# A graph layer's node phase: when turn, product and rows of a group are made, and when gathered rows are stored

## The chip, the cores and the metric

The kernel runs on one core of one Trainium2 chip. The metric is the device time of one execution in microseconds (us). Three runs of the kernel before took 4763.48, 4764.75 and 4766.40 us; the median, 4764.75 us, is its time here.

A core has five engines with queues of their own: PE (matrix products and transposes, with PEld for its weight loads), DVE (vector work), ACT (scalar functions), POOL (here: it issues the gathers) and SP (it issues most other DMAs). An engine takes its instructions in the order of its queue. What orders the engines against each other are semaphores.

## The reference, cut to what matters

There are 12500 nodes with 128 features and 400000 edges, sorted by destination. One graph attention layer (GATv2, 8 heads) and a feed-forward block follow a normalised input:

```python
h = jnp.maximum(_layernorm(x, axis=-1), 0.0)
# inside the layer, with n1 = layernorm(h) * ln1_g + ln1_b
x_l = (n1 @ W_l).reshape(n, H, C)
x_r = (n1 @ W_r).reshape(n, H, C)
m = leaky_relu(x_l[src] + x_r[dst] + e, 0.2)        # e from the edge attributes
alpha = einsum('ehc,hc->eh', m, att)                 # softmax over the edges of a destination
out = segment_sum(x_l[src] * a[:, :, None], dst)     # then bias, residual, feed-forward
```

The change concerns the first part of the work alone: from `x` to `h`, and from `h` to the table of rows `x_l`, which the edges gather by `src`.

## The kernel before, in words

The nodes are padded to 98 tiles of 128. The program has a **node phase**, in which `h` and `x_l` are made for all nodes, and an **edge phase**, which takes the edges 512 at a time: POOL gathers rows of `x_l` from memory (L938), PE, ACT and DVE work out scores and sums. The edge phase needs `x_l` of all nodes in memory, since any edge may point to any node.

In the node phase a *group* is four tiles (25 groups, the last of two tiles; `qs`). A group goes through small steps. The statistics: `x_stats` (DVE, L500: two instructions a tile), `x_mean` (DVE), a square root on ACT (L778) and a reciprocal on DVE (L776) for all groups of a round together, `relu` (ACT, L513: it makes `h` and sums it up), `h_mean` (DVE), `h_square` (ACT, L536), `h_var` (DVE). The product: `h_turn` (PE, L523: four transposes into a PSUM tile `tp`), `h_turned` (L528: the copy to SBUF, on DVE for odd groups, on ACT for even ones), `product` (PE, L549, into a PSUM tile `lr`), `x_l` (DVE, L556: one instruction a tile, and the group's store by SP, L568). For the first group six more steps make its `x_r` (`xr_steps`, L570); `x_r` of the other groups is made in the edge phase.

Beside the groups the phase **gathers raw rows**: for 28 places of the edge list, whose edges are needed in the edge phase, four gathers each (112 in all) bring rows of the input `x` into an SBUF buffer `raw` (`raw_gather`, POOL, L293), and SP stores the buffer in memory (`raw_store`, L305). There are 12 such buffers, so the gathers of place k + 12 wait until the store of place k has landed.

The order is written out by hand. The program is a loop of **rounds** r (L753). In a round come first the raw gathers and stores that are due, then constants (round 3 weights; rounds 9 to 11 and on: differences of destinations, on ACT in rounds 11 to 17, stored by SP in round 18; round 13 constants of the edge phase, DVE; round 15 `fits`, a check on DVE with a small product on PE), then the reciprocals and roots, then the statistics (`sums`, L715: group r - late at step `late`), then the products (`products`, L723), then the first group's `x_r`. Each engine's queue holds its instructions in this order.

Before the change the statistics of group g start in round g, and its turn comes in round `turn_at[g]`, which is 13 + 2g // 3 or, if that is later, g + 5: three groups in two rounds, from 13 on to 29. Copy, product and `x_l` follow one, two and three rounds behind the turn. The stores of places 0 to 4 come three rounds behind their gathers (rounds 3, 4, 5, 6 and 8); place 5 is stored in round 17, and from there one place a round, the last eight of all in the last round, 33 (L749 to L751).

Of the kernel before, what the change touches and what calls it, by code (L numbers as in the profile page):

```python
# [13 lines left out]
F32 = mybir.dt.float32  # L14
# [6 lines left out]
PSUM = bass.MemoryType.PSUM  # L21

P = 128
# [11 lines left out]
KU = 2  # L35
U = KU * P
UP = 2
QP = 4
RU = 14
# [9 lines left out]
XW = P + H  # L49
CX = XW // H  # L50
GN = 4
# [5 lines left out]
RAW_MORE = 6  # L57
RAW_SHIFT = 8
RAW_STEPS = 12
TURN_AT = 13  # L60
BUSY = 5
RAW_BUFS = 12
FREE = 5
BIG = 2.0**126
CAP = 2.0**120

# [66 lines left out]
def raw_pairs(nt, n_edges):  # L133

    n_pr = -(-n_edges // (UP * U))
    at = [xr_round(t, nt, n_edges) + XR_STEPS + 1 for t in range(GN, nt, GN)]
    at = at[:-1] + [r + RAW_SHIFT for r in at[:RAW_MORE]]
    return [(r + RAW_STEPS + AHEAD + 1, r) for r in at if r + RAW_STEPS + AHEAD + 2 < n_pr]
# [11 lines left out]
def tile_gnn(  # L150
# [23 lines left out]
    nc = tc.nc  # L174
# [23 lines left out]
    raw = [{"c": c, "i": i, "round": r, "n": UP * KU} for i, (c, r) in enumerate(raw_pairs(NT, n_edges))]  # L198
# [33 lines left out]
    pre = ExitStack()  # L232
    build = pre.enter_context(tc.tile_pool(name="build", bufs=1))
    rng = pre.enter_context(tc.tile_pool(name="rng", bufs=1))
    node = pre.enter_context(tc.tile_pool(name="node", bufs=3))
    once_ps = pre.enter_context(tc.tile_pool(name="once_ps", bufs=1, space=PSUM))
    tp_ps = pre.enter_context(tc.tile_pool(name="tp_ps", bufs=3, space=PSUM))
    lr_ps = pre.enter_context(tc.tile_pool(name="lr_ps", bufs=3, space=PSUM))


# [9 lines left out]
    def load_weights():  # L250
        nc.scalar.dma_start(wl_sb, w_l)
        nc.scalar.dma_start(wr_sb, w_r)
        nc.scalar.dma_start(g1_c, column(ln1_g))
        nc.scalar.dma_start(b1n_c, column(ln1_b))
# [19 lines left out]
    def load_first():  # L274
        nc.scalar.dma_start(
            src_first,
            bass.AP(tensor=src.tensor, offset=src.offset + raw[0]["c"] * UP * KU, ap=[[NCH * K, P], [1, UP * KU]]),
        )
# [12 lines left out]
            )  # L291

    def raw_gather(d):  # L293
        d["x"] = node.tile([P, UP * KU, P], F32, name="raw", bufs=RAW_BUFS)
        for j in range(d["n"]):
            nc.gpsimd.indirect_dma_start(  # L296
                out=d["x"][:, j, :],
                out_offset=None,
                in_=x,
                in_offset=bass.IndirectOffsetOnAxis(  # L300
                    ap=src_raw[:, d["i"], j : j + 1] if d["i"] > 0 else src_first[:, j : j + 1], axis=0
                ),
            )

    def raw_store(d):  # L305
        nc.sync.dma_start(raw_dram[d["i"], :, 0 : d["n"], :], d["x"][:, 0 : d["n"]])

    def load_x(t0, n):
        if n > 0:
            nc.sync.dma_start(h_sb[:, t0 : t0 + n, :], x_t[:, t0 : t0 + n, :])  # L310
# [104 lines left out]
    def from_first():  # L415
        nc.vector.tensor_copy(df, dc)
        nc.vector.tensor_scalar(nf, df[:, 0:EP:U], -1.0, None, op0=OP.mult)
        nc.vector.memset(dlr[:, :, :, OW:OS], 0.0)
# [15 lines left out]
    def fits():  # L434
# [44 lines left out]
    qs = [  # L479
        {"t0": t, "n": n, "ts": slice(t, t + n), "h": h_sb[:, t : t + n, :], "mean": mean_sb[:, t : t + n]}  # L480
        for t, n in quads
    ]
# [45 lines left out]
    def h_turned(by, odd):  # L528
        def turned(d, r):
            if d["t0"] // GN % 2 == odd:  # L530
                d["hT"] = node.tile([P, GN, P], F32, name="hT", bufs=4)
                by(d["hT"][:, 0 : d["n"]], d["tp"][:, 0 : d["n"]])

        return turned
# [9 lines left out]
    def h_var(d, r):  # L544
        nc.vector.tensor_scalar(root_of(d, r, 1), d["ssq"], 1.0 / P, EPS, op0=OP.mult, op1=OP.add)

    xls = [build.tile([P, GN, XW], F32, name=f"xl{i}") for i in range(4)]

    def product(d, r):  # L549
        d["lr"] = lr_ps.tile([P, GN, P], F32, name="lr")  # L550
# [19 lines left out]
    def xr_steps(pool, bank):  # L570


        def tile_of(d, name, i):
            d[name] = pool.tile([P, GN, P], F32, name=f"xr_{i}")
            return d[name][:, 0 : d["n"]]

        def norm(d):
            off = pool.tile([P, GN], F32, name="xr_off")[:, 0 : d["n"]]
            nc.vector.tensor_mul(off, d["mean"], d["r1"])
            hn = tile_of(d, "hn", 0)  # L580
            for t in range(d["n"]):
# [17 lines left out]

        def times(d):  # L600
            d["b"] = bank()
            for t in range(d["n"]):
                nc.tensor.matmul(
                    d["b"][:, t * P : (t + 1) * P], d["hT"][:, t, :], wr_c.rearrange("p c h -> p (c h)"),
                    start=True, stop=True,
                )

        def keep(d):
            n = d["n"]
            d["xr"] = pool.tile([P, GN, XW], F32, name="xr_rows")[:, 0:n, 0:P]  # L610
# [97 lines left out]
    def clear(g):  # L708
# [3 lines left out]
                empty.rearrange("p h f -> p (h f)")[:, None, :].to_broadcast([P, GT, SW]),  # L712
            )

    sums = (  # L715
        (2, x_mean),
        (4, h_mean),
        (6, h_var),
        (0, x_stats),
        (3, relu),  # L720
        (5, h_square),
    )
    products = (  # L723
        (1, h_turned(nc.vector.tensor_copy, 1)),
        (1, h_turned(nc.scalar.copy, 0)),
        (3, x_l),
        (2, product),
        (0, h_turn),
    )
    turn_at = [TURN_AT + 2 * g // 3 for g in range(len(qs))]  # L730
    turn_at = [max(at, g + 5) for g, at in enumerate(turn_at)]
    XL_AT = turn_at[0] + 3
    END = turn_at[-1] + 4
    first_xr = xr_steps(node, lambda: once_ps.tile([P, GN * P], F32, name="w_ps"))
    with tc.manual_schedule():
        load_first()
        make_identity(nc, ident)
        for t in xls:
            nc.vector.memset(t[:, :, P:], 1.0)
        load_weights()  # L740
        load_x(0, min(GN, NT))
        load_raw()
        load_x(GN, min(3 * GN, NT - GN))
        for t in range(4 * GN, NT, 14):
            load_x(t, min(14, NT - t))
        load_dst()
        load_consts()
        nc.vector.memset(empty, 0.0)
        nc.vector.memset(empty[:, :, C + 1 : SH], CAP)  # L749
        rows_at = [min(i * 5 // 4, END - 1) for i in range(len(raw))]  # L750
        kept_at = [at + 3 if i < FREE else min(XL_AT + 1 + i - FREE, END) for i, at in enumerate(rows_at)]  # L751
        assert all(kept_at[i - RAW_BUFS] <= rows_at[i] for i in range(RAW_BUFS, len(raw)))
        for r in range(max(END, 13 + RU // UP, 16) + 1):  # L753
            if r == 0:
                count_up()
            for d, at, kept in zip(raw, rows_at, kept_at):
                if r == at:
                    raw_gather(d)
                if r == kept:
                    raw_store(d)  # L760
            if r == 3:
                weights()
            if r == 9:
                last_of_units()
            if r == 10:
                from_first()
            if 0 <= r - 11 < RU // UP:
                differ(r - 11)
            if r == 11 + RU // UP:
                keep_differences()  # L770
            if r == 13:
                edge_constants()
            if r == 15:
                fits()
            for t in slots(r - 2):
                nc.vector.reciprocal(t, t)  # L776
            for t in slots(r - 1):
                nc.scalar.activation(t, t, AF.Sqrt)  # L778
            for late, f in sums:
                if 0 <= r - late < len(qs):  # L780
                    f(qs[r - late], r)
            for late, f in products:
                for d, at in zip(qs, turn_at):
                    if r == at + late:
                        f(d, r)
            if 0 <= r - XL_AT < len(first_xr):
                first_xr[r - XL_AT](qs[0])
        clear(0)
    pre.close()

# [1112 lines left out]
```

## Time and profile before

| what | us |
|---|---|
| median of three runs | 4764.75 |
| the profiled execution | 4750.58 |
| its span | 4748.8 |
| first raw gather on POOL starts | 3.42 |
| last raw gather starts | 215.80 |
| last `x_l` instruction of the node phase starts | 220.14 |
| first gather of the edge phase starts | 224.40 |
| first product of a full edge round on PE (L996) | 237.66 |

The profile is of one execution; times count from the start of its span, and the execution has 1.8 us around the span. In lists of instructions each line has the start and the duration in us, engine, line, operation, tiles and shapes, the count, and in brackets how long the engine was idle before it and what ended that ("issue": nothing that the profile shows; "remote": a releaser that it doesn't name). In tables of windows each engine has its busy time and, behind an x, its instructions. In groups by line, the first pair of numbers is busy us and mean ns of one, the rest idle time before them.

### The profile page before, as it was taken

How to read it: one execution, taken by the hardware profiler on the slowest of the kernel's cores; microseconds unless marked ns; L12 is line 12 of the kernel's file. 1: busy time of each engine (PE TensorE's matmuls, PEld its weight loads, DVE VectorE, ACT ScalarE, POOL GpSimd, SP SyncE). 2: the span in 40 equal slices, each digit the busy share in tenths (PEclk: the TensorE clock that was granted, in tenths of full speed). 3: DMA queues.
4: the chain of work that ended last, by engine and by line, in shares of the span. 5: the costliest groups of instructions: out<-in, count | busy, mean ns of one | idle time of the engine just before them, and what ended most of it. 6: DMA issues, size and time to landing. Idle time of an engine off the chain costs nothing.

```text
span 4748.8 us, 63213 instructions
## 1 busy us (share of the span) xinstructions
PE 3809.5 (80%) x18462; PEld 2367.6 (50%) x18463; DVE 2975.0 (63%) x6288; ACT 2166.6 (46%) x4744; POOL 2960.0 (62%) x3140
## 2 busy tenths in 40 slices
PE   0368888888888888888888888888888888888888
PEld 0335555555555555555554555555555555555555
DVE  2647677676676666666666666666666656656655
ACT  3524344344445445445444454444454454444443
POOL 5466666666666666666666666666666666666663
PEclk9779898888899989998998998999899899889898
DMA  5546666555554444444444444444444444444442
GB/s 137 174 120 153 157 160 151 139 137 134 127 116 96 92 93 89 96 84 92 94 95 92 92 101 92 85 95 84 92 99 93 91 90 88 90 89 85 96 89 54
DMA packets 625454, 502.71 MB, mean 106 GB/s; under 512 B 320318, under 2 KB 522157, under 8 KB 624861
## 3 DMA queue, kind: packets, MB, share of 16 engines
q1 hardware_dynamic: 524381, 281.11, 25.5%
q0 software_dynamic: 100000, 217.32, 21.7%
q8 instruction: 153, 2.51, 0.2%
q14 instruction: 200, 1.64, 0.1%
q10 hardware_dynamic: 720, 0.13, 0.0%
HBM read 432.28 MB, written 65.83 MB: 105 GB/s over the span
## 4 chain that ended last, share of the span: by engine, by line
PE 63%; DVE 12%; issue 10%; another core or an unknown queue 7%; ACT 2%; DMA 1%; SPq 0%; POOL 0%; DVEq 0%; ACTq 0%
PE acc L1059 16%; PE ab L1020 14%; PE z L996 13%; PE pt_ps L1045 10%; PE z L992 7%; DVE rec L1026 2%; DVE ea L979 2%; DVE m L1015 2%; DVE own L1068 2%; PE acc L1343 1%; ACT p L1037 1%; PE acc L1368 1%; DVE rec L1074 1%; DVE ne L985 0%
## 5 line engine op out<-in xcount | busy, mean ns | idle before, releaser
L938 POOL DMA_INDIRECT xs<-xl_dram,src_sb x3009 | 2847.6, 946 | 1622.2 <-issue 785.6
L1037 ACT ACTIVATE p<-ab,rec 128x256 f32<-128x256 f32 x1563 | 656.1, 471 | 1254.3 <-DVE rec L1026 781.6
L1059 PE MATMUL acc<-xs,pt 128*128 128x136 f32 x6250 | 1007.4, 307 | 162.7 <-issue 111.7
L1068 DVE TENSOR_TENSOR own<-acc,diag 128x272 f32<-128x272 f32 x782 | 341.5, 437 | 1268.5 <-remote 373.2
L1059 PEld LDWEIGHTS acc<-xs,pt 128*128 128x128 f32 x6250 | 901.5, 214 | 193.5 <-issue 136.1
L996 PE MATMUL z<-ea,zw 64*128 64x512 f32 x1564 | 934.7, 678 | 36.0 <-issue 11.2
L1020 PE MATMUL ab<-m,negrep 128*128 128x512 f32 x1564 | 895.8, 655 | 15.0 <-issue 13.7
L1050 ACT COPY pt<-pt_ps 128x512 f32<-128x512 f32 x782 | 456.3, 584 | 974.3 <-remote 346.9
L992 PEld LDWEIGHTS z<-ident,xs 128*128 128x128 f32 x3125 | 399.7, 151 | 708.1 <-issue 323.1
L992 PE MATMUL z<-ident,xs 128*128 128x128 f32 x3125 | 518.6, 291 | 288.0 <-remote 79.6
L1045 PEld LDWEIGHTS pt_ps<-ident,p 128*128 128x128 f32 x3125 | 357.6, 150 | 739.6 <-issue 668.9
L1045 PE MATMUL pt_ps<-ident,p 128*128 128x128 f32 x3125 | 563.0, 306 | 96.4 <-issue 61.6
L979 DVE TENSOR_SCALAR ea<-dl,nid 32x516 f32<-32x516 bf16 x782 | 582.0, 744 | 32.1 <-issue 6.8
L1015 DVE TENSOR_TENSOR m<-z,zs 128x512 f32<-128x512 f32 x782 | 532.5, 681 | 94.1 <-issue 45.9
L1026 DVE TENSOR_REDUCE rec<-ab 128x2 f32<-128x512 f32 x781 | 533.4, 683 | 71.3 <-remote 35.4
L1010 ACT ACTIVATE zs<-z 128x512 f32<-128x512 f32 x782 | 475.8, 608 | 45.5 <-issue 23.3
L1003 PE MATMUL ab<-ne,farw 64*128 64x512 bf16 x782 | 318.3, 407 | 106.3 <-ACT p L1037 76.4
L1074 DVE TENSOR_REDUCE rec<-own 128x34 f32<-128x272 f32 x782 | 340.8, 436 | 26.8
L996 PEld LDWEIGHTS z<-ea,zw 64*128 64x128 f32 x1564 | 245.3, 195 | 198.2 <-issue 178.2
L1020 PEld LDWEIGHTS ab<-m,negrep 128*128 128x128 f32 x1564 | 276.4, 216 | 30.4 <-issue 30.0
L296 POOL DMA_INDIRECT raw<-in_x,src_raw x112 | 105.9, 946 | 102.5 <-DMA raw_dram<-raw 67.7
L985 DVE TENSOR_SCALAR ne<-dl,nid 96x512 bf16<-96x512 bf16 x391 | 150.0, 384 | 13.4 <-DMA dl<-du_dram 1.0
(232 smaller groups left out, 2195.3 us busy)
## 6 DMA issues: line engine op xcount, KB each, us to landing
ea<-in_ea_t SPq DMA_DIRECT2D x392, 128.0 KB
ea_s<-in_ea_t SPq DMA_DIRECT2D x98, 512.0 KB
xs<-xl_dram,src_sb POOLq DMA_INDIRECT x3009
dl<-dc_dram SPq DMA_DIRECT2D x392, 66.0 KB
state<-rec SPq DMA_DIRECT2D x1563, 9.0 KB
state<-empty SPq DMA_DIRECT2D x28, 504.0 KB
f_st<-state SPq DMA_DIRECT2D x46, 288.0 KB
dl<-du_dram SPq DMA_DIRECT2D x392, 32.0 KB
```

The source lines that it names most:

```text
L938: nc.gpsimd.indirect_dma_start(out=xs[:, j, :], out_offset=None, in_=xl_dram, in_offset=bass.IndirectOffsetOnAxis(ap=src_sb[:, c * KP + j ...
L979: nc.vector.tensor_scalar(d["ea"][rs].rearrange("p (a b) -> p a b", b=OW), d["dl"][rs].rearrange("p (a b) -> p a b", b=OS)[:, :, 0:OW], ni ...
L992: nc.tensor.matmul(z[:, j * P : (j + 1) * P], d["xs"][:, j, 0:P], ident, start=(j == 0), stop=False, is_transpose=True)
L996: nc.tensor.matmul(z[:, :e], d["zw"][rs], d["ea"][rs, :e], start=False, stop=True)
L1010: nc.scalar.activation(d["zs"][:, :e], d["z"][:, :e], AF.Copy, scale=SLOPE)
L1015: nc.vector.tensor_tensor(d["m"][:, :e], d["z"][:, :e], d["zs"][:, :e], op=OP.max)
L1020: nc.tensor.matmul(d["ab"][:, :e], negrep.rearrange("p n h -> p (n h)"), d["m"][:, :e], start=False, stop=True)
L1026: nc.vector.tensor_reduce(d["rec"][:, :, CX], d["ab"].rearrange("p (u e) -> p u e", e=U), AX.X, OP.min)
L1037: nc.scalar.activation(d["p"][:, us], d["ab"][:, us], AF.Exp, bias=d["rec"][:, i, CX:SH], scale=-1.0)
L1045: nc.tensor.transpose(d["pt_ps"][:, js], d["p"][:, js], ident)
L1050: nc.scalar.copy(d["pt"][:, :e], d["pt_ps"][:, :e])
L1059: nc.tensor.matmul(d["acc"][:, i, :], d["pt"][:, j * P : (j + 1) * P], d["xs"][:, j, :], start=(j == js[0]), stop=(j == js[-1]),)
```

## The change

The products join the statistics in one list with fixed distances. The turn of group g comes in round g + 4, its copy in g + 5, its product in g + 7, its `x_l` in g + 8: one group a round, the first `x_l` in round 8 and the last in round 32. Within a round `x_l`, `product` and `h_turn` stand behind the copy of odd groups and ahead of `relu`; the copy of even groups on ACT stands last. Every place's raw rows are stored three rounds behind their gathers: places 5 to 15 in rounds 9, 10, 11, 13, 14, 15, 16, 18, 19, 20 and 21, the last four in rounds 33 to 36. The loop has 37 rounds and had 34. The steps for the first group's `x_r` start in round 8 and started in round 16. The PSUM pool of `tp` has two tiles and had three; the buffers of `x_l` are three and were four. No instruction is added or taken away, and the sizes of all are the same.

```diff
-    tp_ps = pre.enter_context(tc.tile_pool(name="tp_ps", bufs=3, space=PSUM))
+    tp_ps = pre.enter_context(tc.tile_pool(name="tp_ps", bufs=2, space=PSUM))
...
-    xls = [build.tile([P, GN, XW], F32, name=f"xl{i}") for i in range(4)]
+    xls = [build.tile([P, GN, XW], F32, name=f"xl{i}") for i in range(3)]
...
-    sums = (
+    node_stages = (
         (2, x_mean),
         (4, h_mean),
         (6, h_var),
         (0, x_stats),
+        (5, h_turned(nc.vector.tensor_copy, 1)),
+        (8, x_l),
+        (7, product),
+        (4, h_turn),
         (3, relu),
         (5, h_square),
+        (5, h_turned(nc.scalar.copy, 0)),
     )
-    products = (
-        (1, h_turned(nc.vector.tensor_copy, 1)),
-        (1, h_turned(nc.scalar.copy, 0)),
-        (3, x_l),
-        (2, product),
-        (0, h_turn),
-    )
-    turn_at = [TURN_AT + 2 * g // 3 for g in range(len(qs))]
-    turn_at = [max(at, g + 5) for g, at in enumerate(turn_at)]
-    XL_AT = turn_at[0] + 3
-    END = turn_at[-1] + 4
+    LAST = 8
...
-        rows_at = [min(i * 5 // 4, END - 1) for i in range(len(raw))]
-        kept_at = [at + 3 if i < FREE else min(XL_AT + 1 + i - FREE, END) for i, at in enumerate(rows_at)]
...
-        for r in range(max(END, 13 + RU // UP, 16) + 1):
+        rows_at = [i * 5 // 4 for i in range(len(raw))]
+        for r in range(max(max(len(qs), 9) + LAST + 1, max(12 + RU // UP, 16), rows_at[-1] + 4)):
...
-                if r == kept:
+                if r == at + 3:
                     raw_store(d)
...
-            for late, f in sums:
+            for late, f in node_stages:
                 if 0 <= r - late < len(qs):
                     f(qs[r - late], r)
-            for late, f in products:
-                for d, at in zip(qs, turn_at):
-                    if r == at + late:
-                        f(d, r)
-            if 0 <= r - XL_AT < len(first_xr):
-                first_xr[r - XL_AT](qs[0])
+            if 0 <= r - LAST < len(first_xr):
+                first_xr[r - LAST](qs[0])
```

More of the change, by code (lines that the diff above doesn't have):

```diff
@@ L59 @@
 RAW_STEPS = 12
-TURN_AT = 13
 BUSY = 5
-RAW_BUFS = 12
-FREE = 5
 BIG = 2.0**126
@@ L293, in raw_gather @@
     def raw_gather(d):
-        d["x"] = node.tile([P, UP * KU, P], F32, name="raw", bufs=RAW_BUFS)
+        d["x"] = node.tile([P, UP * KU, P], F32, name="raw", bufs=12)
         for j in range(d["n"]):
@@ L749, in tile_gnn @@
         nc.vector.memset(empty[:, :, C + 1 : SH], CAP)
-        rows_at = [min(i * 5 // 4, END - 1) for i in range(len(raw))]
-        kept_at = [at + 3 if i < FREE else min(XL_AT + 1 + i - FREE, END) for i, at in enumerate(rows_at)]
-        assert all(kept_at[i - RAW_BUFS] <= rows_at[i] for i in range(RAW_BUFS, len(raw)))
-        for r in range(max(END, 13 + RU // UP, 16) + 1):
+        rows_at = [i * 5 // 4 for i in range(len(raw))]
+        for r in range(max(max(len(qs), 9) + LAST + 1, max(12 + RU // UP, 16), rows_at[-1] + 4)):
             if r == 0:
                 count_up()
-            for d, at, kept in zip(raw, rows_at, kept_at):
+            for d, at in zip(raw, rows_at):
                 if r == at:
                     raw_gather(d)
-                if r == kept:
+                if r == at + 3:
                     raw_store(d)
```

## The prediction

> **What bounds the kernel now.** The page comes first, to see how much of the run the change can touch.
>
> ```profile
> span 4748.8 us, 63213 instructions
> ...
> PE   0368888888888888888888888888888888888888
> ...
> L296 POOL DMA_INDIRECT raw<-in_x,src_raw x112 | 105.9, 946 | 102.5 <-DMA raw_dram<-raw 67.7
> ```
>
> A slice of the PE row is 118.7 us (4748.8 / 40). PE is full from the third or fourth slice on; the change edits the node phase alone, which lies in the first two. The third line is the other user of that phase: 112 gathers of raw rows on POOL (four more have a group of their own). They cost POOL 106 us, and POOL waited 67.7 us for a buffer to be stored. So I read the phase by windows, cut where the timeline changes its pace.
>
> ```profile
> core 0: us, PE busy (x) PEld busy (x) DVE busy (x) ACT busy (x) POOL busy (x), PEclk, DMA share, GB/s
> ...
> 19.00:99.00 80.00, 3.80 (x8) 1.46 (x8) 9.80 (x62) 18.67 (x74) 52.53 (x56) 1.00 0.58 141
> 99.00:131.00 32.00, 0.00 (x0) 0.00 (x0) 26.96 (x120) 32.00 (x134) 0.00 (x0) 1.00 0.00 1
> 131.00:165.00 34.00, 23.67 (x158) 21.93 (x158) 28.86 (x147) 32.08 (x132) 13.50 (x15) 0.90 0.59 185
> 165.00:180.00 15.00, 2.50 (x12) 2.54 (x13) 4.30 (x20) 5.68 (x21) 9.22 (x10) 0.57 0.40 118
> ...
> 190.00:203.00 13.00, 1.97 (x11) 1.76 (x9) 3.23 (x13) 6.75 (x30) 9.25 (x10) 0.67 0.37 109
> ```
>
> Two paces show. From 99 to 165 ACT is busy 64 of 66 us: ACT sets the pace. From 19 to 99, 165 to 180 and 190 to 203 no engine but POOL is busy, and few instructions are issued: **slow stretches**. The timeline tells what they wait for.
>
> ```profile
> 73.76 0.18 DVE L505 BATCH_NORM_AGGREGATE n_stats<-s 128x2 f32<-128x6 f32 x1 [2.44 <-issue]
> 84.93 0.20 ACT L515 ACTIVATION_READ_ACCUMULATOR h_sb<-h_sb,n_m,roots_sb 128x1 f32 x1 [0.90 <-issue]
> 86.33 0.49 ACT L515 ACTIVATE h_sb<-h_sb,n_m,roots_sb 128x128 f32<-128x128 f32 x1 [1.20 <-issue]
> 98.96 0.40 ACT L540 ACTIVATE sq<-h_sb,mean_sb 128x128 f32<-128x128 f32 x1 [1.23 <-ACT sq L540]
> 165.10 0.18 DVE L505 BATCH_NORM_AGGREGATE n_stats<-s 128x2 f32<-128x6 f32 x1 [0.34 <-DVE s L504]
> 177.50 3.61 PE L552 MATMUL lr<-wl_c,hT 128*128 128x128 f32 x16 [12.58 <-remote]
> 218.45 0.37 ACT L532 COPY hT<-tp 128x256 f32<-128x256 f32 x1 [8.83 <-remote]
> ```
>
> Inside a stretch an instruction comes every 1.4 us (ACT at 84.93 and 86.33), with no releaser in the profile. POOL's own timeline has the other half.
>
> ```profile
> 3.42 1.10 POOL L296 DMA_INDIRECT raw<-in_x,src_first  x1 [0.22 <-DMA src_first<-in_src]
> 88.77 0.95 POOL L296 DMA_INDIRECT raw<-in_x,src_raw  x1 [0.30 <-issue]
> 142.86 0.95 POOL L296 DMA_INDIRECT raw<-in_x,src_raw  x1 [53.15 <-DMA raw_dram<-raw]
> 157.25 0.94 POOL L296 DMA_INDIRECT raw<-in_x,src_raw  x1 [4.68 <-DMA raw_dram<-raw]
> 176.02 0.95 POOL L296 DMA_INDIRECT raw<-in_x,src_raw  x1 [0.30 <-issue]
> 207.03 0.95 POOL L296 DMA_INDIRECT raw<-in_x,src_raw  x1 [3.83 <-DMA raw_dram<-raw]
> 224.40 0.95 POOL L938 DMA_INDIRECT xs<-xl_dram,src_sb  x1 [7.66 <-DMA raw_dram<-raw]
> 283.17 0.95 POOL L938 DMA_INDIRECT xs<-xl_dram,src_sb  x1 [0.30 <-issue]
> ```
>
> Gathers issue every 1.25 us (0.95 + 0.30). Suppose that something behind them needs 1.4 us for each (an estimate, fitted to these rows). A run of 68 from 3.42 would be worked off at 3.42 + 95.2 = 98.6; the last wait of ACT ends at 98.96. A run of 16 from 157.25 (to 176.02) ends at 179.7 by this; PE came back at 177.50. A run of 8 from 207.03 ends at 218.2; ACT's wait ended at 218.45. The stretch that follows 157.25 began at 165.10, 7.9 us or some seven gathers in. So my rule for this phase: **a run of n gathers without a pause makes a slow stretch from about 7.5 us after its start to 1.4 n us after it.** POOL stood still from 89.7 to 142.9 because the sixth store waits in SP's queue for round 17: that is what bought the fast window 99 to 142.
>
> **The change part by part.** What it removes, adds and moves: no arithmetic changes. Moved forward are 25 turns, copies, products and rows, the first group's x_r, 25 stores of x_l and 23 stores of raw rows. The stores are all on SP: x_l's now go one a round ahead of the loads and stores that the constants add to that queue (lu in round 9, the differences in round 18), which nothing needs before the edge phase or the check of round 15.
>
> *Rounds 0 to 8.* Stores 0 to 4 keep their rounds, so 17 groups of four gathers go out as before, POOL stops at 89.7 and the stretch ends at 99. Inside it rounds 5 to 8 now carry two copies and four row instructions more on DVE. At 1.4 us each (row 86.33) that is 8.4 us; what is left at 99 goes at the fast pace, so I take 5: round 9 starts at 102 and not at 97. Bounds: 1 us, if only busy time counts, and 8 us, if PE in the loop holds up whole rounds as it does in the edge phase's first stretch:
>
> ```profile
> 47.86 0.16 DVE L509 SCALAR_TENSOR_TENSOR n_m<-n_stats,roots_sb 128x4 f32<-128x4 f32 x1 [2.55 <-remote]
> 65.36 0.16 DVE L509 SCALAR_TENSOR_TENSOR n_m<-n_stats,roots_sb 128x4 f32<-128x4 f32 x1 [2.55 <-remote]
> ...
> 260.15 1.08 PE L992 MATMUL z<-ident,xs 128*128 128x128 f32 x4 [9.16 <-issue]
> 285.35 1.08 PE L992 MATMUL z<-ident,xs 128*128 128x128 f32 x4 [19.36 <-issue]
> ```
>
> The edge round took 25.2 us (285.35 - 260.15); a node round without work for PE took 17.5 (65.36 - 47.86, the same step of two rounds). At 25.2 us rounds 5, 6 and most of 7 fit ahead of 99, and 8 us are lost.
>
> *Rounds 9 to 32 at the fast pace.* The costs:
>
> ```profile
> L560 DVE SCALAR_TENSOR_TENSOR xl<-lr,roots_sb,bl_r 128x128 f32<-128x128 f32 x98 | 26.9, 341 | 8.3 <-remote 7.9 <-PE lr L552 0.4
> L532 DVE COPY hT<-tp 128x512 f32<-128x512 f32 x12 | 8.2, 685 | 16.5 <-remote 16.5
> L532 ACT COPY hT<-tp 128x512 f32<-128x512 f32 (+1 forms) x13 | 7.2, 552 | 15.3 <-remote 15.3
> ```
>
> ```profile
> 97.00:143.00 46.00, 10.31 (x66) 9.71 (x66) 38.30 (x182) 43.19 (x172) 0.14 (x1) 1.00 0.06 18
> 143.00:222.00 79.00, 35.03 (x230) 31.61 (x230) 44.01 (x203) 48.04 (x209) 45.29 (x48) 0.76 0.62 191
> ```
>
> 97 to 143 is rounds 9 to 17: DVE 38.3 us, ACT 43.2. These rounds held 12 row instructions and now hold 36: 24 x 0.274 (26.9 / 98) = 6.6 us more for DVE, and one copy more, 0.7: 45.6. DVE passes ACT and bounds them. With the 2.8 us that the pace setter idled before (46.0 - 43.2): 48.4. Behind them ACT's 48.0 us bound, less four copies (4 x 0.55 = 2.2) and what moves ahead of x_r (1.4): 44.4, and 2.3 us from the last copy (218.45) to the end of the last row (220.75). Sum 48.4 + 44.4 + 2.3 = 95. PE's bursts hide behind both: its busy time in these two windows is 45 us (10.3 + 35.0). Two PSUM tiles for turns and three for rows cost nothing here: a tile is asked for again two rounds (some 8 us) later, and copied out one round later; they cost a round's wait inside a stretch, when ACT or SP is late.
>
> *Slow stretches after 102.* Store k frees the buffer of group k + 12. Stores 5 to 15 go in rounds 9, 10, 11, 13, 14, 15, 16, 18, 19, 20, 21, each behind the x_l of the round before it, where they went in rounds 17 to 27. The 44 late gathers are no fewer. Groups of rounds 9 to 11 make a run of 12: 16.8 - 7.5 = 9.3 us of stretch. Round 13 is long (constants) and stands alone: 0. Rounds 14 to 16 have the check of round 15 in between: a run of 8, 11.2 - 7.5 = 4 (of 12, 9). Rounds 18 to 21 make 16: 22.4 - 7.5 = 14.9. Together 28 us. In the two stretches shown (28 us) ACT did 12.4 us of work and DVE 7.5, so 56% to 73% is lost; I take 70%, near DVE: 20 us. Bounds 5 and 39 are the rivals'.
>
> *The end.* The order was x_l's last row, store, POOL's first edge gather:
>
> ```profile
> 220.14 0.61 DVE L560 SCALAR_TENSOR_TENSOR xl<-lr,roots_sb,bl_r 128x128 f32<-128x128 f32 x2 [0.40 <-PE lr L552]
> 221.32 4.96 SPq L306 DMA_DIRECT2D raw_dram<-raw  x8
> ```
>
> Four raw stores stay behind the last row instead of these eight, 2.5 us of SP. I cost that at nothing: PE's start is steered by the 48 gathers from 224.40 to 283.17, which by the rule hold the other engines until 224.4 + 67.2 = 291.6, and POOL's start needs the rows to land (bounds: -2.5 and 0).
>
> **The sum.** 102 + 95 + 20 = 217 for the last row, which was at 220.75: 3.75 us earlier, and everything behind it with it. The profiled execution took 4750.6 us (span 4748.8), 14 us under the median 4764.75, so I carry the difference over: 4761.0. Its own bounds: 98 + 95 + 16 = 209, or 105 + 95 + 28 = 228, so -12 to +7: 4753 to 4772. What a measurement of this kernel can tell from no change is about 0.2%, 9.5 us.
>
> A rule of the Trainium skill speaks another way. On its page "SBUF — State Buffer", section "Who interferes with whom", DVE and GpSimd share a port pair and only they hold each other up; "PE and ACT never wait on anyone". ACT's 1.20 us wait beside running gathers (row 86.33) disagrees, unless its cause is another than ports. By that rule the gathers cost ACT nothing, and the only new price would be copies of DVE that hold up POOL.
>
> **Rivals.**
>
> *Faster: the runs break.* 4 gathers need 5.6 us by the rule; a round gives 0.8 of a group, so rounds over 4.5 us (5.6 / 1.25) leave a pause each time. Rounds 9 to 17 average 5.4. Then 5 us are lost and not 20: last row at 202, -19: 4746. For it: the 8 gathers from 142.86 left ACT at 32 us of 34 (131 to 165). Against it: rounds 18 on come at 3.7 us (44.4 over 12 rounds of ACT).
>
> *Slower: the runs join.* If rounds 9 to 21 stay under 4.5 us where it counts, or POOL has buffers in hand, all 44 gathers become one run: 61.6 - 7.5 = 54 us of stretch, 73% lost is 39; with round 9 at 105: 105 + 95 + 39 = 239, +18: 4783. It decides where a group of four is freed every 5.6 us or sooner. For it: POOL now gets buffers from round 9, with ACT and DVE both full, and PE's chain in each round, as in 165 to 180. Against it: a stretch slows the rounds that free the buffers.
>
> *No stretch at all, as the port rule would have it.* Last row at 102 + 95 = 197: -24: 4741. The rows 86.33, 98.96 and 218.45 speak against.
>
> *Nothing moves*, as the end of the phase waits for a landing that has its own time: 4764.75.
>
> **How the numbers follow.** Forecast 0.43, runs break 0.20, runs join 0.30, no stretch 0.03, nothing 0.04. The range takes in both rivals' centres, 4741 to 4783. Faster by over 0.2%: 0.20 + 0.03 and 0.06 of the forecast's own spread, 0.29. Slower: 0.30. Within: the rest, 0.41.
>
> **What would show it.** Round 9 (the copy lu) at about 102 and not 97; POOL's second run beginning near 105 and not at 142.86; DVE busier than ACT from 102 to 150; POOL's last raw gather before 195; x_l's last row near 217. It is wrong if the windows 105 to 165 look like 165 to 180 throughout, or if the row ends at 200.

## The result, and the profile after

The kernel after took 4743.4 us (median of 6 runs, 4733.35 to 4744.10), the kernel before 4765.6 beside it (6 runs): a ratio of 0.9948 (95% interval 0.9936 to 0.9961), 22 us less. The forecast was 4761, no difference to be measured. 4743 lies at the low end of the range, next to the rival "the runs break" (4746). This program was met in two conditions, one in which the kernel before takes 4755 to 4830 us, as here, and one in which it takes 3961 to 3973 us and the traces show no slow stretch (two chips were seen in both), and each kernel is compared only with the kernel before on the same chip at the same time.

The profiled execution of the kernel after took 4739.06 us, 4 under its median; that of the kernel before lay 14 under its own. So the two traces are 11.5 us apart where the medians are 22. First the page after:

```profile
span 4737.3 us, 63216 instructions
...
PE   2468888888888888888888888888888888888887
...
L293 POOL DMA_INDIRECT raw<-in_x,src_raw x112 | 110.1, 983 | 65.7 <-issue 35.4 <-DMA raw_dram<-raw 29.5 <-DMA raw<-in_x,src_raw 0.8
```

Of its 65.7 us of idle time before these gathers POOL waited 29.5 for stores of raw rows; before, it was 67.7 of 102.5. Windows of the kernel after, cut as for the kernel before:

```profile
19.00:99.00 80.00, 11.68 (x44) 8.99 (x44) 12.70 (x72) 21.59 (x80) 52.52 (x56) 0.64 0.59 143
99.00:131.00 32.00, 17.03 (x72) 13.96 (x72) 25.60 (x116) 29.64 (x115) 17.12 (x16) 0.55 0.36 109
131.00:165.00 34.00, 15.24 (x87) 13.16 (x88) 29.29 (x139) 30.24 (x130) 18.46 (x17) 0.72 0.60 190
165.00:180.00 15.00, 5.18 (x32) 4.29 (x32) 7.63 (x41) 9.73 (x43) 11.34 (x12) 0.80 0.50 144
190.00:203.00 13.00, 8.72 (x49) 8.27 (x49) 7.70 (x35) 13.00 (x64) 0.00 (x0) 0.76 0.48 157
```

From 99 to 165 ACT is nearly as full as before (59.9 us of 66, then 64.1) although POOL now gathers in these windows (35.6 us busy, then 13.5). What POOL does there it need not do later: from 190 to 203 it is idle, and ACT is full where it had 6.75 us. POOL's own list shows the runs:

```profile
89.44 0.94 POOL L293 DMA_INDIRECT raw<-in_x,src_raw  x1 [0.30 <-issue]
101.64 2.96 POOL L293 DMA_INDIRECT raw<-in_x,src_raw  x1 [11.26 <-DMA raw_dram<-raw]
124.28 0.94 POOL L293 DMA_INDIRECT raw<-in_x,src_raw  x1 [5.96 <-DMA raw_dram<-raw]
135.09 3.38 POOL L293 DMA_INDIRECT raw<-in_x,src_raw  x1 [6.11 <-DMA raw_dram<-raw]
163.85 0.94 POOL L293 DMA_INDIRECT raw<-in_x,src_raw  x1 [2.67 <-DMA raw_dram<-raw]
183.30 0.94 POOL L293 DMA_INDIRECT raw<-in_x,src_raw  x1 [0.30 <-issue]
210.44 0.94 POOL L924 DMA_INDIRECT xs<-xl_dram,src_sb  x1 [26.20 <-DMA raw_dram<-raw]
```

68 gathers to 89.4, a pause of 11 us, then runs of 12, 4, 8, 4, 4 and 16. The edge phase starts at 210.44 (224.40 before). DVE's list shows the start of round 9, what is left of the slow stretches, and the last row:

```profile
90.21 0.68 DVE L529 COPY hT<-tp 128x512 f32<-128x512 f32 x1
90.81 1.12 DVE L557 SCALAR_TENSOR_TENSOR xl<-lr,roots_sb,bl_r 128x128 f32<-128x128 f32 x4
91.84 0.15 DVE L576 TENSOR_TENSOR xr_off<-mean_sb,roots_sb 128x4 f32<-128x4 f32 x1
92.20 0.18 DVE L404 COPY lu<-dc 112x14 int32<-112x14 int32 x1 [0.20 <-issue]
98.58 0.16 DVE L506 SCALAR_TENSOR_TENSOR n_m<-n_stats,roots_sb 128x4 f32<-128x4 f32 x1 [4.77 <-remote]
116.95 0.17 DVE L503 TENSOR_SCALAR roots_sb<-n_stats 128x4 f32<-128x4 f32 x1 [1.55 <-remote]
177.99 0.18 DVE L502 BATCH_NORM_AGGREGATE n_stats<-s 128x2 f32<-128x6 f32 x1 [3.68 <-remote]
184.29 0.18 DVE L502 BATCH_NORM_AGGREGATE n_stats<-s 128x2 f32<-128x6 f32 x1 [1.74 <-remote]
205.94 0.61 DVE L557 SCALAR_TENSOR_TENSOR xl<-lr,roots_sb,bl_r 128x128 f32<-128x128 f32 x2
```

The last row starts at 205.94 and ends at 206.55 (220.14 and 220.75 before; 217 was the forecast for its end). One copy and four rows, which I had put at 1.4 us each in the first stretch, took 1.7 us together (90.21 to 91.93). One row of ACT from the last slow stretch, for the pace in it:

```profile
180.06 0.40 ACT L537 ACTIVATE sq<-h_sb,mean_sb 128x128 f32<-128x128 f32 x1 [1.20 <-issue]
```

ACT still waits 1.20 us with no releaser in the profile.

### The profile page after: what moved, and what is told of

Its sections match the earlier page's. It is cut to its first block, busy times and chain, and to the rows that moved or that the text cites. A ratio compares the mean times of both kernels' runs of the same rounds, so it can differ in the third digit from the quotient of the medians.

```text
span 4737.3 us, 63216 instructions
## 1 busy us (share of the span) xinstructions
PE 3825.7 (81%) x18462; PEld 2377.5 (50%) x18463; DVE 2973.9 (63%) x6287; ACT 2165.7 (46%) x4744; POOL 2957.2 (62%) x3140
## 4 chain that ended last, share of the span: by engine, by line
PE 59%; DVE 13%; issue 11%; another core or an unknown queue 7%; ACT 2%; POOL 2%; DMA 1%; SPq 1%; DVEq 0%; POOLq 0%; ACTq 0%
PE acc L1045 15%; PE ab L1006 12%; PE z L982 12%; PE pt_ps L1031 9%; PE z L978 7%; DVE rec L1012 3%; POOL xs L924 2%; DVE ea L965 2%; DVE m L1001 2%; DVE own L1054 2%; PE acc L1329 1%; ACT p L1023 1%; PE acc L1354 1%; DVE rec L1060 1%
## 5 line engine op out<-in xcount | busy, mean ns | idle before, releaser
L982 PE MATMUL z<-ea,zw 64*128 64x512 f32 x1564 | 934.5, 678 | 42.3 <-issue 15.8
L1006 PE MATMUL ab<-m,negrep 128*128 128x512 f32 x1564 | 895.1, 654 | 19.2 <-issue 17.3
L293 POOL DMA_INDIRECT raw<-in_x,src_raw x112 | 110.1, 983 | 65.7 <-issue 35.4
```

The costliest lines, as they stand in the source:

```text
L982: nc.tensor.matmul(z[:, :e], d["zw"][rs], d["ea"][rs, :e], start=False, stop=True)
L1006: nc.tensor.matmul(d["ab"][:, :e], negrep.rearrange("p n h -> p (n h)"), d["m"][:, :e], start=False, stop=True)
```

## Experiments

The theories. **A**: slow stretches come from runs of gathers that issue faster than something behind them takes them, 1.4 us each; the stores of raw rows set the runs. **B**: the early products bring the gain, as they fill rounds 9 to 17. **C**: the hold-up goes by the bytes or the number of gathers, not their pace. Later, when each part alone had moved nothing: **E**, the two parts need each other, since the early x_l stores on SP's queue hold back the raw stores; **F**, early products are needed for their own sake.

**The pace of the gathers.** A POOL memset of a private tile behind each raw gather of the changed kernel:

```diff
+            nc.gpsimd.memset(pace, 0.0)      # behind each indirect_dma_start of raw_gather
```

128x128 first (a gather every 1.34 us), alone and with the first 48 gathers of the edge phase:

> The changed kernel with one small POOL memset (128x128, 0.20 us in the trace) behind each raw gather, so that gathers issue every 1.45 us or so and not every 1.25. Theory A (something behind the gathers needs about 1.4 us for each, and a run faster than that holds up the handoffs of all engines): no slow stretch is left; the copy of round 9 comes before 70 us (92.2 in the changed kernel), POOL's last raw gather near 175 to 190, the last row between 180 and 195 (206), and the time falls by 12 to 25 us against the changed kernel. Theory C (the hold-up goes by the bytes that the gathers move, or by their number, not by their pace): the stretch from 19 to 99 is stretched to 19 to 110 or longer, round 9 comes at 100 or later, and the time rises by 0 to 20 us.

> As the last one, and the first 48 gathers of the edge phase (12 pairs of tiles in four gathers each, which go out in one run of 60 us) are spaced by the same memset. Theory A: PE's gaps of 20.0 and 12.2 us after 241 us in the changed kernel go; the first edge rounds follow each other every 6 us, so some 5 rounds are made earlier: 15 to 30 us less than with the raw gathers alone spaced. Theory C: PE waits as long as before or longer, within 5 us of the last one or slower.

Measured, where the kernel before takes 3963 us: 3972.7 (1.0027, 1.0016 to 1.0037) and 3977.3 (1.0037, 1.0023 to 1.0051). There was nothing to win: in this condition ACT is busy 61 to 71 of the 80 us from 19 to 99 in every trace (the part "One part alone" shows one). 116 gathers x 0.09 us is 10 us later, as measured, and neither A nor C is tested. Then 128x384, with the changed kernel as its base:

> The changed kernel itself beside the kernel before, as a base for the others on the chip of this call. On a chip where the kernel before takes 4765 us, theories A and B both expect 16 to 24 us less. On a chip where it takes 3963 us (the four runs above: no slow stretch, ACT busy 68 of 80 us from 19 to 99, POOL's raw gathers without a pause to 156, and the last row at 141, ahead of POOL's end), theory A expects that POOL's 116 gathers set the start of the edge phase, so that the change is worth nothing: within 5 us of the kernel before, the last raw gather at 156 to 160. Theory B expects the products' 14 us there too.

> The changed kernel with a POOL memset of 128x384 behind each raw gather: with 128x128 a gather came every 1.34 us (0.95 + 0.17 + 0.22), with this one every 1.5 to 1.6. On a chip where the kernel before takes 4765 us: theory A (a run of gathers faster than 1.4 us each holds up the handoffs) expects no slow stretch, the copy of round 9 before 70 us, the last row between 180 and 200 and 10 to 25 us less than the changed kernel; theory C (it goes by bytes or by number) expects the stretch to last as long or longer and 0 to 30 us more. On a chip where it takes 3963 us, POOL's own pace ends the phase: 116 x 0.3 = 35 us more than the changed kernel, the last raw gather near 190.

Measured, with the kernel before at 4762.3: the changed kernel 4739.3 (0.9949, 0.9937 to 0.9961), the paced one 4725.9 (0.9913, 0.9900 to 0.9927). The paced one's window and a part of POOL's list:

```profile
19.00:99.00 80.00, 33.40 (x162) 28.19 (x162) 59.08 (x266) 62.14 (x254) 72.13 (x95) 0.68 0.73 191
```

```profile
59.76 0.95 POOL L295 DMA_INDIRECT raw<-in_x,src_raw  x1 [0.17 <-issue]
60.71 0.43 POOL L303 MEMSET pace<- 128x384 f32 x1
61.30 0.95 POOL L295 DMA_INDIRECT raw<-in_x,src_raw  x1 [0.17 <-issue]
...
190.48 0.95 POOL L927 DMA_INDIRECT xs<-xl_dram,src_sb  x1 [0.34 <-issue]
```

The same gathers of the same bytes, one every 1.55 us instead of 1.25, and ACT is busy 62.1 us of 80 instead of 21.6 (19.2 in the changed kernel beside it). DVE's list has round 9's copy and the last row:

```profile
38.82 0.29 DVE L407 COPY lu<-dc 112x14 int32<-112x14 int32 x1 [3.07 <-issue]
150.82 0.61 DVE L560 SCALAR_TENSOR_TENSOR xl<-lr,roots_sb,bl_r 128x128 f32<-128x128 f32 x2 [4.99 <-DMA xl_dram<-xl]
```

The last row is sooner than A's 180 to 200, the time as A said. **It is the pace.** C falls. What ends the phase now is POOL itself, at 190. Next, 128x256 (one gather every 1.44 us), with the first 48 gathers of the edge phase and then with all 3009:

> The changed kernel with a POOL memset of 128x256 behind each raw gather and behind each of the first 48 gathers of the edge phase, so that one goes out every 1.45 us (0.95 + 0.17 + an estimated 0.33, between the measured 0.22 and 0.43 for 128x128 and 128x384). Where the kernel before takes 4765 us, theory A: the raw gathers end near 178 (188.8 at 1.55 us each), the edge phase starts near 180, and PE's gaps in the first edge rounds (20 and 12 us in the changed kernel) go: 4680 to 4710, 15 to 45 us less than with the raw gathers alone spaced at 1.55 us (4725.9). Theory C (spacing the raw gathers helped by leaving DMA queues or memory to the loads of x, not by the 1.4 us): the edge gathers' spacing gains nothing, 4715 to 4735. Where the kernel before takes 3963 us: 10 to 30 us more than it.

> As the last one, with the memset behind all 3009 gathers of the edge phase. They go out in runs of eight at 1.25 us with a pause of 2 us behind each, 1.5 us each on average, and PE shows waits of 0.4 to 1.3 us with no releaser in the second half of such runs. Theory A, where the kernel before takes 4765 us: spaced at 1.45 us no run is ahead of the 1.4 us, the waits go, and the time falls by another 50 to 200 us (PE is busy 840 of 1000 us, and its gaps of 160 are what can be gained of some 4500). Theory D (PE's own chain of products sets the edge phase, and gathers only fill its pauses): within 20 us of the last one. Where the kernel before takes 3963 us, POOL ends last: 3009 x 0.2 = 600 us less the pauses, some 400 us more.

Measured: 4710.0 (0.9889, 0.9874 to 0.9905) and 4694.9 (0.9863, 0.9844 to 0.9882) beside 4762.0. The first met its number, but not all of its picture: from 107 on ACT waits again, for PE's turns, and a gap of PE in the edge phase is left.

```profile
137.49 0.59 ACT L532 COPY hT<-tp 128x512 f32<-128x512 f32 x1 [8.87 <-remote]
276.96 1.09 PE L983 MATMUL z<-ident,xs 128*128 128x128 f32 x4 [12.19 <-issue]
```

The first row is one of the waits that begin when some 70 gathers are out. At 1.4 us a gather there should be none at a spacing of 1.44, so either that figure is a little low or these waits have another cause; the run doesn't tell which. The gap of the second row stands behind the 48 paced gathers, when the next ones go out at 1.25 us again. The second kernel gained 15 us and not 50 to 200: theory D's number, though a pace of 1.44 us that is still too fast would look the same; the run doesn't tell. Both beat the kernels before and after; where the kernel before takes 3963 us they were not run, and the spacing cost 10 to 14 us there already at 1.34 us.

**One part alone.** The kernel before with the early stores, and the changed kernel with the late ones:

```diff
# early_stores, in the kernel before
-        rows_at = [min(i * 5 // 4, END - 1) for i in range(len(raw))]
-        kept_at = [at + 3 if i < FREE else min(XL_AT + 1 + i - FREE, END) for i, at in enumerate(rows_at)]
+        rows_at = [i * 5 // 4 for i in range(len(raw))]
+        kept_at = [at + 3 for at in rows_at]
...
# held_stores, in the changed kernel
-        rows_at = [i * 5 // 4 for i in range(len(raw))]
+        rows_at = [min(i * 5 // 4, 32) for i in range(len(raw))]
+        kept_at = [at + 3 if i < 5 else min(12 + i, 33) for i, at in enumerate(rows_at)]
...
-                if r == at + 3:
+                if r == kept:
                     raw_store(d)
```

> The kernel before with one part of the change alone: every place's raw rows are stored three rounds behind their gathers; turns, products and rows stay late. Theory A (the phase costs ACT's work plus the time lost in slow stretches, and the stores set how the gathers fall into runs): the 44 late gathers begin near 101 us and not at 142.9, the stretches cost about as much as in the changed kernel (14 us, where the kernel before lost 32 on ACT from 99 to 222), and the last row of x_l starts at 206 to 210 instead of 220.1; the time falls by 10 to 15 us against the kernel before. Theory B (the gain comes from the products that fill the rounds 9 to 17): the last row stays within 4 us of 220 and the time within 5 us of the kernel before.

> The changed kernel with the raw rows stored as before the change (places 5 and on from round 17, one a round, eight in round 33); turns, products and rows stay early. Theory A: rounds 9 to 17 run without a slow stretch (about 48 us), then the gathers come in the runs of the kernel before (from round 17 to the end), ACT loses 15 us or more from 150 on, and the last row starts at 212 or later; the time is 6 to 15 us above the changed kernel. Theory B: the last row starts near 206 as in the changed kernel, and the time is within 5 us of it.

Measured first with the kernel before at 3962.9: 3963.9 (1.0002, 0.9993 to 1.0011) and 3966.5 (1.0010, 1.0001 to 1.0019). The window of the first shows why nothing could come of it, and POOL's list what ends the phase:

```profile
19.00:99.00 80.00, 18.82 (x100) 15.81 (x101) 55.41 (x276) 68.10 (x286) 59.26 (x58) 0.96 0.76 204
```

```profile
156.04 0.94 POOL L296 DMA_INDIRECT raw<-in_x,src_raw  x1 [0.30 <-issue]
157.29 0.95 POOL L938 DMA_INDIRECT xs<-xl_dram,src_sb  x1 [0.30 <-issue]
```

Gathers at 1.25 us hold up nobody here (ACT 68.1 us of 80), and the edge phase begins the moment POOL has issued its 116. Then again, with the kernel before at 4762.0:

> The kernel before with the early stores alone, once more, for a chip where the kernel before takes 4765 us. Theory A: the late gathers begin near 101 us, the last row of x_l starts at 204 to 212 (220.1 before) and the time falls by 8 to 20 us against the kernel before. Theory B: the last row within 4 us of 220, the time within 5 us of the kernel before. Where the kernel before takes 3963 us: as in the first run, within 3 us of it.

> The changed kernel with the stores held as before, once more, for a chip where the kernel before takes 4765 us. Theory A: no slow stretch from 99 to about 150, the stretches of the kernel before after that, the last row at 212 or later, and 6 to 15 us more than the changed kernel (4739). Theory B: the last row near 204 and within 5 us of it. Where the kernel before takes 3963 us: 2 to 5 us more than it, as in the first run.

Measured: 4755.8 (0.9993, 0.9979 to 1.0006) and 4762.5 (0.9998, 0.9989 to 1.0007). **Neither part alone moves the time**; the early stores missed A's number, the early products B's. The early products alone lay 23 us above the changed kernel, where A had said 6 to 15. The traces say why. Early stores alone, DVE and POOL:

```profile
137.52 0.17 DVE L545 TENSOR_SCALAR roots_sb<-n_ssq 128x4 f32<-128x4 f32 x1 [1.99 <-ACT sq L540]
```

```profile
126.16 0.94 POOL L296 DMA_INDIRECT raw<-in_x,src_raw  x1 [0.31 <-issue]
177.68 0.95 POOL L296 DMA_INDIRECT raw<-in_x,src_raw  x1 [50.57 <-DMA raw_dram<-raw]
```

POOL made 96 gathers without the pause at 68: the runs joined, the rival on the slower side of my prediction (the expectation of gated_early below says 92 gathers and a stretch to 131; this trace has 96 and 137.5). The rule puts the end of the stretch at 3.46 + 96 x 1.4 = 137.9; the last long wait ended at 137.5. The last row came at 232.2. With the late stores in the changed kernel POOL stood still until 148.68 and made its 48 late gathers after that, beside the rounds that were left:

```profile
148.68 0.94 POOL L293 DMA_INDIRECT raw<-in_x,src_raw  x1 [59.02 <-DMA raw_dram<-raw]
```

Its last row came at 224.4. So why don't the runs join in the changed kernel? Its SP queue has the answer:

```profile
97.83 0.39 SPq L565 DMA_DIRECT2D xl_dram<-xl  x1
98.48 0.29 SPq L303 DMA_DIRECT2D raw_dram<-raw  x1
```

The store of round 8's x_l stands ahead of the raw store of round 9. DVE had those rows made by 91.93, but the store leaves SP only at 97.83, near the end of the stretch, so the raw store goes at 98.48, and POOL goes on at 101.64. From there each raw store stands behind the x_l store of a round. In the early stores alone nothing of the kind stood ahead, and the same raw store was the last of six that were out by 71.6:

```profile
49.93 21.70 SPq L306 DMA_DIRECT2D raw_dram<-raw  x6
```

That is theory E, and two kernels test it: the early stores alone with something small in the place of the x_l stores, and the changed kernel with the raw stores let go ahead of them.

```diff
# gated_early: early_stores, and this
         nc.vector.tensor_scalar(d["mean"], d["mean"], -1.0 / P, None, op0=OP.mult)
+
+        if r >= 8:
+            nc.sync.dma_start(gate[0:1, d["t0"] : d["t0"] + d["n"]], d["mean"][0:1, :])
...
# ungated_after, in the changed kernel
-        rows_at = [i * 5 // 4 for i in range(len(raw))]
+        rows_at = [i if i < 5 else i * 5 // 4 - 2 if i < 16 else i * 5 // 4 for i in range(len(raw))]
+        kept_at = [i * 5 // 4 - 2 if 5 <= i < 16 else i * 5 // 4 + 3 for i in range(len(raw))]
...
-                if r == at + 3:
+                if r == kept:
                     raw_store(d)
```

> The kernel before with the early stores alone, and from round 8 on one 16-byte DMA a round of a group's mean on SP's queue (into a scratch place), which waits for that round's DVE work as the store of x_l does in the changed kernel; turns, products and rows stay late. In the run early_stores_b nothing held SP's queue back, POOL went on from 68 gathers to 92 without a pause, and the slow stretch lasted to 131. Theory E (the two parts need each other: the early x_l stores on SP's queue hold the raw stores to one a round, and that breaks the gathers into short runs; the early products bring nothing else): POOL stops near 90 and goes on near 101 to 105, ACT is busy 50 of 66 us or more from 99 to 165, the last row of x_l starts at 203 to 214, and the time falls by 7 to 20 us against the kernel before. Theory F (early products are needed for their own sake, since they fill DVE and PE while ACT sets the pace): the last row at 216 or later, the time within 6 us of the kernel before. Where the kernel before takes 3963 us: within 4 us of it by both.

> The changed kernel with its raw stores of places 5 to 15 emitted five rounds earlier (rounds 4 to 16), so that on SP's queue they stand ahead of the x_l stores of five rounds; turns, products and rows stay early. Theory E: POOL does not stop at 68 gathers but goes on to 84 or more, the slow stretch lasts to 115 to 130 instead of 99, the last row starts at 214 or later (204 to 206 in the changed kernel), and most of the change's 22 us is lost: 4750 to 4770 where the kernel before takes 4762. Theory F: the last row within 4 us of the changed kernel's and the time within 6 us of it (4739 to 4743). Where the kernel before takes 3963 us: within 5 us of it by both.

Measured twice where the kernel before takes 3971 us: 0.9999 and 1.0000 for the first, 0.9996 and 0.9999 for the second (intervals of 0.0009 to either side), and beside the second pair the changed kernel itself:

> The changed kernel as it is, as a base for these two on their chip. Where the kernel before takes about 4762 us: 18 to 28 us less, as twice before. Where it takes some 3970 us, both theories expect nothing: within 5 us of it, since POOL's 116 gathers without a pause end the node phase there (156 us) and the last row is made before (141 us).

3969.9, 0.9998 (0.9989 to 1.0007): **in this condition the change is worth nothing**. Then in the other condition, the kernel before at 4802.7 for the first and at 4819.1 for the two others:

> As gated_early and gated_early_b, for a chip where the kernel before takes about 4762 us. Theory E: POOL stops near 90 and goes on at 101 to 105, the last row of x_l starts at 203 to 214, and the time falls by 7 to 20 us against the kernel before. Theory F: the last row at 216 or later, the time within 6 us. Where the kernel before takes some 3970 us: within 4 us of it by both, as twice before.

> As ungated_after, for a chip where the kernel before takes 4760 to 4800 us and slow stretches exist. Theory E: POOL goes on to 84 gathers or more without a pause, the slow stretch lasts to 115 to 130, the last row starts at 214 or later, and the time is 10 us or more above the changed kernel's. Theory F: within 6 us of it, the last row near 204. Where the kernel before takes some 3970 us: within 5 us of it by both, as twice before.

> The changed kernel as a base on the same chip: 0.9945 to 0.9955 of the kernel before where slow stretches exist. What it has beyond the 0.9971 of the early stores with a held queue (about 10 us) is what the early products bring of their own (in theory E by what they take out of the rounds after 165, where turns, copies and rows came three groups in two rounds). Where the kernel before takes some 3970 us: within 5 us of it, as once before.

Measured: the gated one 4788.8 (0.9971, 0.9960 to 0.9982), the ungated one 4810.7 (0.9980, 0.9971 to 0.9989), the changed kernel 4800.2 (0.9964, 0.9952 to 0.9976). POOL and DVE of the gated one:

```profile
103.59 0.94 POOL L297 DMA_INDIRECT raw<-in_x,src_raw  x1 [0.31 <-issue]
112.48 0.94 POOL L297 DMA_INDIRECT raw<-in_x,src_raw  x1 [7.95 <-DMA raw_dram<-raw]
```

```profile
110.55 0.17 DVE L549 TENSOR_SCALAR roots_sb<-n_ssq 128x4 f32<-128x4 f32 x1 [2.44 <-ACT sq L544]
```

The 16-byte DMAs broke the run at 76 gathers where it had been 96; the stretch ended near 110.5 (3.41 + 76 x 1.4 = 109.8), the last row came at 216.3 (outside of E's 203 to 214), and the time fell by 14 us with the products as late as before. By E POOL would have stopped near 90 already, and a last row at 216 or later is F's sign; the time is E's. Beside the early stores alone the edge phase started 15 us sooner (221.61 and 236.69, on two chips). The ungated one, POOL and DVE:

```profile
108.57 0.94 POOL L293 DMA_INDIRECT raw<-in_x,src_raw  x1 [0.30 <-issue]
114.33 0.94 POOL L293 DMA_INDIRECT raw<-in_x,src_raw  x1 [4.82 <-DMA raw_dram<-raw]
```

```profile
127.32 0.18 DVE L502 BATCH_NORM_AGGREGATE n_stats<-s 128x2 f32<-128x6 f32 x1 [1.05 <-DVE s L501]
```

84 gathers in the first run and four more behind a short pause, long waits to 127 (3.41 + 88 x 1.4 = 126.6), the last row at 218.5 (208.9 in the changed kernel beside it), and 10.5 us more than the changed kernel; the edge phase started 9.6 us later than in it (223.01 and 213.39, on the same chip). By their ratios the intervals of these two overlap a little. So the ungated kernel met E's numbers in all points, the gated one in its broken run and its time. E does not explain all: in ratios, the gated kernel has 0.0029 and the changed one 0.0036 to 0.0052, with intervals that partly overlap. What is left, 3 to 11 us, may be the shorter first run (68 against 76) or the early products; that stays open. The changed kernel itself gained less here than the 0.9945 to 0.9955 that was expected.

## Why the prediction was wrong, point by point

Its mechanism held, but no net change was forecast because three terms were mis-sized: the stretches behind round 9 (20 us lost, 13 measured), the five us for rounds 0 to 8 (nothing measured) and the 14 us carried over from the trace to the median (4 measured).

*The bound and the rule: right in the main.* In this condition the phase is ACT's work and the time lost in slow stretches, and 1.4 us a gather put the ends of the first stretches of five kernels to within 1 us (one of them is the kernel that it was fitted on). The pace experiment shows that the pace of the gathers makes the stretches; the figure of 1.4 stays a fit, which the waits at 1.44 don't bear out. What it is behind the gathers that takes this time was not found. That DVE would pass ACT in rounds 9 to 17 was wrong: from 102 to 150 ACT was busy 42.3 us and DVE 39.6.

*Rounds 0 to 8, five us: wrong.* I multiplied six instructions by 1.4 us. In a stretch not all instructions come 1.4 us apart: ACT's own successive ones do (84.93 and 86.33 before), while DVE's copy and four rows took 1.7 us together (above). What makes the difference is not shown. Round 9's copy came at 92.2, 100.7 and 94.6 in three traces of the changed kernel, 97.0 before: the term is nothing, to within 5 us. The statistics behind it ran on at 98.6 (98.98 before).

*The dense rounds, 95 us: about right.* From 98.6 to 206.5 are 108 us; less the 13 or so that the stretches took (below), 95.

*Slow stretches after 102, 28 us with 20 lost: the term of the trace that failed most.* The trace has stretches at some 116.5 to 120.5, at 148 to 155 in two short pieces, and at 172 to 184.5: 19 us, of which some 13 were lost (12.5 for one round that takes 3.6 without, and 4 in the others). The step that was wrong is the one lead of 7.5 us that I gave every run before it is felt. I took it from the run that starts at 157.25 in the kernel before. The first run of all, in the same fence, needed 15.6 us (3.42 to 19), and the run of 12 after the change 14.9 (101.64 to 116.5), so my 9.3 us for that run were four. For the last run, of 16, the lead was some 8 us (163.85 to 172). Why it is 15 in one place and 8 in another is open: a debt from the run before does not explain it, since the run from 148.68 in the changed kernel with late stores follows 59 us of rest and is felt after some 10. The 4 us for rounds 14 to 16 (the two short pieces) and the 0 for round 13 were near. A count was off too: the traces have 29 stores and 116 gathers of raw rows, so there are 29 places and not 28, 48 late gathers and not 44, and after the change 39 rounds, with five stores behind the last row.

*The rivals.* "The runs break" had its place and its price nearly right (row 202, 4746; measured 206.5 and 4743) and got 0.20, though its price is near by luck, as it holds the 14 us carried over; its threshold, a pause after each group, was stricter than need be. "The runs join" was real as well, in the early stores alone: what I had not seen is that x_l's stores on SP's queue decide between the two. I named that order ("each behind the x_l of the round before it") and priced it at nothing. "No stretch at all" has a time close to the result, 4741, for a reason that isn't there: ACT still waits 1.20 us beside the gathers (row 180.06), as it did before the change. By the Trainium skill's page "SBUF — State Buffer", section "Who interferes with whom", ACT would wait for no one; the trace disagrees, unless the cause is another than ports, which it doesn't tell.

*The end of the phase: right.* The edge phase started 14.0 us earlier, with the last row 14.2 us earlier.

*The sum against the median: open.* 14 us of the start become 11.5 at the end of the two traces and 22 between the medians. The profiled execution of the kernel before was quicker than all six measured beside the change, and I carried its distance from the median over as a constant. Of the 17.6 us between forecast and median, 9.8 are this constant (14.2 carried over, 4.3 measured); the other 7.8 are the last row's end, 10.5 us sooner than 217, less 2.7 lost behind it. The other kernels point at the trace of the kernel before as well: in seven traces (three of the changed kernel, and the kernels early_stores_b, held_stores_b, gated_early_c and ungated_after_c) the time fell by 5 to 19 us more than the start of the edge phase moved against this one trace. That would fit an execution whose edge phase began sooner than usual. There is no second trace of that kernel in this condition, so it is not shown.

## What to carry to other kernels

Here gathers that issued every 1.25 us slowed down every engine, and the remedy was their pace, not their amount: look at how long the runs of such a producer are, and what breaks them. When two parts of a change each do nothing alone, look for the queue on which one part stands ahead of the other. Check a rule against every event in the fence, not the one that it was fitted on, before pricing with it. And take a second trace of the kernel before, where its one trace lies 14 us from the median.

## What the runs showed of the hardware

- In one condition 128-row gathers issued every 1.25 us held up the instructions of ACT, DVE and PE after some 12 in a row (after 7 or so in some runs); at 1.55 us each the hold-up was gone, and at 1.44 us there were waits after about 70, whose cause is not settled. In the other condition, gathers at 1.25 us held up nobody, and the whole kernel took 3963 us instead of 4765, with a granted clock of some 0.955 instead of 0.90. One chip showed 3963 and later 4803 for the kernel before, another 3971 and later 4819; what puts it in one condition or the other is not known.
- A POOL memset between gathers cost less than its own time: the idle time before the next gather fell from 0.30 to 0.17 us, so 0.22 us of memset added 0.09 us to the cadence.
- One DMA of 16 bytes a round that waits for DVE, ahead of the raw stores on SP's queue, broke a run of gathers at 76 instead of 96. The early stores took 0.9993 of the kernel before without it and 0.9971 with it.
